# Four fetch buffers for the transposed scores, and the rest of the sum added in pieces

## The chip, the cores and the metric

The kernel runs on one core of one Trainium2 chip. The metric is the device time of one execution in microseconds (us), and lower is better. The engines are named as in the profile: PE (TensorE, the matmuls), DVE (VectorE), ACT (ScalarE), POOL (GpSimd) and SP (SyncE, which here only issues DMAs). Each engine has its own instruction queue and works through it in order.

## The reference

For x of shape [2, 2048, 256], the kernel computes attention and a gated feed-forward net (FFN) side by side on the same normalised input, and adds both to x:

```python
xn = _layernorm(x, axis=-1)
x = x + _L0_attn_ref(xn, Wq, Wk, Wv, Wo) + _L0_ffn_ref(xn, w1_w, w1_s, ..., w3_w, w3_s)
...
# attention: one head of width 256, causal
q, k, v = x @ Wq, x @ Wk, x @ Wv
attn = softmax(where(causal_mask, -max, q k^T) * 256 ** -0.5)
out = (attn v) @ Wo
...
# FFN, hidden width 1024; every weight is -1, 0 or 1, with a scale for each output
h = silu(tlin(x, w1)) * tlin(x, w2)
h = gelu(tlin(h, h1)); h = gelu(tlin(h, h2))
return tlin(h, w3)
```

## The kernel before, in words

**Tiles.** The 4096 rows are eight blocks n of TB = 512 rows, four (NB) for each batch, and each block is four tiles t of 128 rows; "(2,3)" is block 2, tile 3. Matmul operands are fp32r pairs: a rounded high half and the remainder as a low half, made by a copy on ACT (hi) and a subtraction on DVE or POOL (lo). A product is three products of halves.

**Attention.** Keys, queries and values of a block are made at L363 to L398 (the queries' projection is folded into wqk, the output's into wvo). `score` (L407 to L446) makes the scores of one tile against the blocks of its batch up to its own (PE L425, the mask L431), reduces the maxima (DVE L434, L440) and takes the exponential on ACT (L446), with the row sums. The tiles of batch 0 run from (3,3) down to (0,0), those of batch 1 upward from (4,0).

**Turning P.** The exponentials P must stand transposed ahead of the product with the values. A tile's P is cut into units of up to UK = 8 blocks of 128 columns. A unit of at least five goes "by blocks": DVE transposes 32x32 squares into one of two b tiles (L308), SP stores it to DRAM as d (L313), and four DMAs on SP fetch it back rearranged into a buffer e (L320). e comes from the pool bp with two buffers. `turn` (L470) then makes a piece pT of up to four blocks: ACT copies the hi half (L484), and DVE (even m) or POOL (odd m) subtracts for the lo half (L486). pT comes from the pool ptp, with LEAD + 2 = 4 buffers. Smaller units and the last tile are transposed on PE (L490) and split by ACT (L264) and DVE (L265). `weigh` (L505) multiplies by the values: hi products L518, lo products L523, into one of two PSUM tiles po; ACT L533 and DVE L537 (with L529 and L531) normalise into r, which is stored as r_d. `fetch_units` issues the fetches out of the list of stored units when `turn` reaches the first piece of a unit, and then one unit ahead. `weigh_steps` puts the turns LEAD = 2 pieces ahead of the weighing.

**Beside it.** x of batch 1 is loaded, normalised on POOL (L345, scale and offset from DVE L300) and turned in the same way by the b tiles (`turn_keys`, L351, so L308 and L313 also read x and write d_x). Between the steps, `beside` issues checks of the FFN's weights in small steps (DMA on ACT's queue L661; L590 to L607 on ACT and DVE, among them L603 and L605) and the sums of h1's quarters (`sum_up`, L611), which are gathered in the tile xh0 and stored to DRAM. Those begin after the last check of h2's signs. The pool xp has four buffers for x. At the end of attention the first parts of the FFN's gate are already made (`first_quarter`, L174 with ACT L182 and DVE L183).

**FFN.** `ffn_ternary` works on pairs of blocks. The gate (L174, L182, L183, splits L187 and L188) gives quarters B11, B12, B21 and B22. Each of the two hidden layers, `square`, is one Strassen step: seven products of 32 matmuls (L883), with sums and differences on DVE and POOL between them (L858, L863, L864, L922). The last product (L1044) gives y, and DVE adds it to "rest", x plus attention, and stores it. `rests_of` (L1004), called behind product 3 of the second layer, fetches attention's result and x (L1013, L1014) and adds them on POOL: L1015, one add of 128x1024 for each block, eight in all.

**What sets the order.** The order of issue in the source is not the order on the engines: each engine's queue is laid out by a scheduler from its own model of the times. `issue_after(x)` gives an edge to x only to instructions on x's own engine. The lists `looks`, `extra`, `TURN_KEYS` and the constants AHEAD, DELAY and LEAD say in which order the source issues.

```python
def fetch_units(until, more):
    while units and (more or until not in fetched):
        more = more and until not in fetched
        n, t, u, k, d = units.pop(0)
        e = bp.tile([P, UK * P], F32, tag="e", name=f"e_{n}_{t}_{u}")[:, : k * P]
        fetched[n, t, u] = fetch_blocks(d, k, e)
```

Of the kernel before, what the change touches and what calls it, by code (L numbers as in the profile page):

```python
# [20 lines left out]
P = 128  # L21
# [11 lines left out]
LOOKS_FROM = 3  # L33
LEAD = 2
WARM = 26
WARM_KEYS = 6
# [29 lines left out]
def attn_ffn_kernel(  # L66
# [124 lines left out]
    with ExitStack() as actx:  # L191
# [6 lines left out]
        sp = actx.enter_context(tc.tile_pool(name="sp", bufs=3))  # L198
        bp = actx.enter_context(tc.tile_pool(name="bp", bufs=2))
        ptp = actx.enter_context(tc.tile_pool(name="ptp", bufs=LEAD + 2))  # L200
        small = actx.enter_context(tc.tile_pool(name="small", bufs=4))
# [3 lines left out]
        xs, rstds, ks, qs, vs = {}, {}, {}, {}, {}  # L205
        turns = {"ps": 0, "b": 0, "q": 0}

        def in_turn(key, tiles):
            turns[key] += 1
            return tiles[(turns[key] - 1) % len(tiles)]  # L210

        def bank():
# [249 lines left out]

        def fetch_units(until, more):
            while units and (more or until not in fetched):
                more = more and until not in fetched
                n, t, u, k, d = units.pop(0)
                e = bp.tile([P, UK * P], F32, tag="e", name=f"e_{n}_{t}_{u}")[:, : k * P]
                fetched[n, t, u] = fetch_blocks(d, k, e)

        def turn(n, t, m):  # L470

            first = n - n % NB
            tiles = NT if m < n else t + 1
            w = tiles * P
            pT = ptp.tile([P, 2, TB], F32R, tag="pT", name=f"pT_{n}_{t}_{m}")
            state[n, t][m] = pT
            if by_blocks(n, t, m):
                u, at = divmod((m - first) * NT, UK)
                fetch_units((n, t, u * UK), at == 0)
                src = fetched[n, t, u * UK][:, ds(at, tiles)]  # L480
                hi, lo = (
                    pT[:, a, :w].rearrange("p (k i q) -> p k i q", k=tiles, q=Q) for a in range(2)
                )
                nc.scalar.copy(hi, src)  # L484
                engine = nc.gpsimd if m % 2 else nc.vector
                engine.tensor_tensor(lo, src, hi.bitcast(F32), ALU.subtract)  # L486
                return
            pt = ps_t.tile([P, TB], F32, tag="pt", name=f"pt_{n}_{t}_{m}")
            for j in range(tiles):
                nc.tensor.transpose(  # L490
                    pt[:, ts(j, P)], state[n, t]["s"][:, ds((m - first) * TB + j * P, P)], ident
                )
            hi_lo(pT[:, 0, :w], pT[:, 1, :w], pt[:, :w])
# [58 lines left out]
        def weigh_steps(g, until):  # L552

            steps = []
            while g < len(blocks) and blocks[g][0] <= until:
                while turned[0] <= min(g + LEAD, len(blocks) - 1) and (
                    turned[0] <= g or blocks[turned[0]][0] <= until + 1
                ):
                    b = blocks[turned[0]]
                    steps.append((0 if by_blocks(*b[1:]) else 2 * TB, lambda b=b: turn(*b[1:])))  # L560
                    turned[0] += 1
                _, n, t, m = blocks[g]
                steps.append((6 * TB if m < n else 6 * P * (t + 1), lambda b=blocks[g]: weigh(*b[1:])))
                g += 1
            return g, steps
# [63 lines left out]

        def item_signs(src):  # L630
            items.append(([src], [(0, lambda t: odd(t[0]))]))

# [17 lines left out]
        for k in range(HC):  # L650
            item_signs(h2[:, k, :])
        for c in range(HK):
# [132 lines left out]
    def ffn_ternary(actx):  # L785
# [83 lines left out]
        def square(layer, n, B, sets, last, beside):  # L869
# [6 lines left out]
            def product(step, out, start):  # L876
# [3 lines left out]
                for o in range(HK):  # L880
                    for c in range(HK):
                        for a in range(2):
                            nc.tensor.matmul(  # L883
                                out=out[o], lhsT=w[:, c, ts(o, P)], rhs=sets[right][c][:, a, :],
                                start=(start and c == 0 and a == 0), stop=(c == HK - 1 and a == 1),
                                skip_group_check=True,
                            )
                if step in beside:
# [57 lines left out]
            return C, nxt  # L946

        raw_h2 = {}

# [54 lines left out]
        def rests_of(n):  # L1004
# [4 lines left out]
            )  # L1009
            rests = {}  # L1010
            for i, m in enumerate((n + 1, n)):
                rests[m] = rest = rt[:, ts(i, NT), :]
                nc.sync.dma_start(out=rest, in_=r_d[m].rearrange("p (t d) -> p t d", d=D))  # L1013
                nc.sync.dma_start(out=xt[:, ts(i, NT), :], in_=rows_of(m))  # L1014
                nc.gpsimd.tensor_tensor(rest, rest, xt[:, ts(i, NT), :], ALU.add)  # L1015
            return rests

# [5 lines left out]
        for n in range(0, N, 2):  # L1023
# [6 lines left out]
            B, sets = square("h1", n, B, sets, False, later)  # L1030
            rests = {}
            B, sets = square("h2", n, B, sets, True, {3: lambda: rests.update(rests_of(n))})
            for m in (n + 1, n):
# [221 lines left out]
```

## Time and profile before

| what | value |
|---|---|
| three runs | 869.96, 867.01, 870.21 us (median 869.96) |
| profiled execution | 868.75 us, its span 866.9 us |
| mean granted PE clock | 0.998 |
| DVE, ACT, POOL busy | 74%, 58%, 27% of the span |
| attention, with the weights' checks | up to about 262 us |
| FFN, four pairs of blocks | from there to the end |
| DMA d<-b (stores of P's units) | 18 of 512 KB, median 3.9 us from issue to landing |
| DMA e<-d (fetches) | 72 of 128 KB, median 3.2 us |

A line of a timeline has the start in us from the beginning of the span, the length, the engine, the source line, the operation, output and inputs by the program's names (numbers left out), the shapes and the count of like instructions in a row; in brackets stands the idle time of the engine ahead of it and what ended that. A line of the waits has the engine and the line that waited, what released it, the total in us, the number of times and the longest. "PEclk" is the share of full clock that PE was granted.

### The profile page before, as it was taken

Reading aid. Unit: us, or ns where it says so; the run is one execution under the profiler, and the core shown is the slowest. Engines: PE = TensorE matmul, PEld = TensorE weight load, DVE = VectorE, ACT = ScalarE, POOL = GpSimd, SP = SyncE. Lnnn points to the kernel's source line nnn. Section 1 sums busy time; section 2 is a strip of 40 time slices with the busy share of each in tenths; the row PEclk is TensorE's granted clock in tenths of the full one; section 3 lists DMA queues with packets and bytes.
Section 4 is the critical chain, followed back from the end, with each engine's and each line's share of the span. In section 5 each row is a group of like instructions: output and inputs, shape, how many; then the busy total and the mean of one; then the engine's idle time right before and its main releaser. Section 6 shows DMA issues by size and latency. Waiting matters only on the chain.

```text
span 866.9 us, 12257 instructions
## 1 busy us (share of the span) xinstructions
PE 849.5 (98%) x4298; PEld 720.5 (83%) x4298; DVE 644.1 (74%) x1123; ACT 498.7 (58%) x881; POOL 234.7 (27%) x178
## 2 busy tenths in 40 slices
PE   9999799999999999999999999999999999999997
PEld 7988688988888878878988888988888898888887
DVE  6689685887965799986596596479478648848764
ACT  3456665655655466676257576436557635557671
POOL 3022823111111666630142150026024003502300
PEclk9999999999999999999999999999999999999999
DMA  8987899667881998754234444433444431144411
GB/s 276 361 233 233 249 314 291 222 234 231 286 283 51 389 403 282 285 194 152 93 132 143 144 146 141 144 116 109 145 145 145 145 135 58 49 146 146 146 49 53
DMA packets 62678, 162.51 MB, mean 187 GB/s; under 512 B 6545, under 2 KB 36369, under 8 KB 53265
## 3 DMA queue, kind: packets, MB, share of 16 engines
q1 hardware_dynamic: 57792, 145.14, 48.6%
q10 hardware_dynamic: 3728, 12.32, 4.6%
q0 software_dynamic: 1088, 4.19, 1.3%
q8 instruction: 36, 0.59, 0.3%
q14 instruction: 34, 0.27, 0.1%
HBM read 120.21 MB, written 47.71 MB: 194 GB/s over the span
## 4 chain that ended last, share of the span: by engine, by line
PE 83%; DVE 6%; DMA 5%; issue 2%; POOL 1%; ACT 1%; SPq 1%; DVEq 0%; ACTq 0%; POOLq 0%
PE ps_own L883 22%; PE ps L883 21%; PE ps L425 7%; PE ps L174 6%; PE ps_own L174 6%; PE po L518 4%; PE ps_own L1044 4%; PE ps L1044 4%; PE ps L398 3%; DMA e<-d 3%; DMA d<-b 2%; PE po L523 2%; PE ps L382 1%; POOL x L345 1%; DVE h_T L188 1%
## 5 line engine op out<-in xcount | busy, mean ns | idle before, releaser
L425 PE MATMUL ps<-k,q 128*128 128x512 f32 (+3 forms) x480 | 109.0, 366 | 0.4 <-ACT q L264 0.4
L425 PEld LDWEIGHTS ps<-k,q 128*128 128x128 f32 x480 | 82.0, 189 | 13.4 <-ACT q L264 1.2
L518 PE MATMUL po<-v,pT 128*128 128x512 f32 x272 | 79.1, 401 | 6.5 <-ACT pT L484 4.7
L486 POOL TENSOR_TENSOR pT<-e,pT 128x512 fp32r<-128x512 f32 (+3 forms) x30 | 36.8, 1229 | 140.1 <-ACT pT L484 102.6
L1015 POOL TENSOR_TENSOR rt<-rt,xt 128x1024 f32<-128x1024 f32 x8 | 21.9, 2758 | 170.3 <-issue 114.8
L904 ACT ACTIVATE k_h_u<-k_h_u,h_s_sb 128x512 f32<-128x512 f32 x64 | 45.9, 723 | 36.6 <-DVE k_h_u L903 36.0
L446 ACT ACTIVATE s<-s,low 128x1024 f32<-128x1024 f32 (+7 forms) x48 | 42.9, 895 | 30.8 <-DVE low L440 30.6
L518 PEld LDWEIGHTS po<-v,pT 128*128 128x128 f32 x272 | 47.3, 189 | 14.3 <-ACT pT L484 5.5
L863 POOL TENSOR_TENSOR k_h_u<-k_h_p,k_h_u 128x512 f32<-128x512 f32 x16 | 23.3, 1459 | 122.1 <-ACT q L187 106.0
L484 ACT CAST pT<-e 128x512 fp32r<-128x512 f32 (+3 forms) x60 | 32.8, 574 | 38.8 <-DMA e<-d 26.9
L434 DVE TENSOR_SCALAR_CACHE_REDUCE s<-ps 128x512 f32<-128x512 f32 (+3 forms) x80 | 47.2, 598 | 5.0 <-PE pt L490 3.1
L523 PEld LDWEIGHTS po<-v,pT 128*128 128x128 f32 x272 | 42.4, 188 | 6.8 <-DVE pT L486 0.7
L523 PE MATMUL po<-v,pT 128*128 128x256 f32 x272 | 46.2, 283 | 0.1
L188 DVE TENSOR_TENSOR q<-k_h_u,q 128x512 fp32r<-128x512 f32 x32 | 43.4, 1384 | 0.0
L308 DVE STREAM_TRANSPOSE b<-s 128x1024 f32<-128x1024 f32 (+3 forms) x30 | 33.4, 1124 | 8.3 <-ACT s L446 4.8
L922 POOL TENSOR_TENSOR k_h_p<-f_h_B,k_h_p 128x512 f32<-128x512 f32 x16 | 32.6, 2065 | 20.0 <-DVE h_h_T L188 20.0
L174 PE MATMUL ps<-xh,w_sb 128*128 128x512 f32 x144 | 36.4, 391 | 0.8 <-ACT b L182 0.8
L863 POOL TENSOR_TENSOR f_w_B<-f_w_B,f_w_B 128x512 f32<-128x512 f32 x16 | 26.8, 1692 | 33.1 <-DVE f_w_B L183 33.1
L903 DVE TENSOR_TENSOR k_h_u<-ps_own,k_h_u 128x512 f32<-128x512 f32 x32 | 21.7, 686 | 17.5 <-PE ps_own L883 17.4
L904 ACT ACTIVATE k_h_p<-k_h_p,h_s_sb 128x512 f32<-128x512 f32 x32 | 22.8, 722 | 19.3 <-DVE k_h_p L903 19.3
L903 DVE TENSOR_TENSOR k_h_u<-ps,k_h_u 128x512 f32<-128x512 f32 x32 | 22.0, 690 | 14.3 <-PE ps L883 14.3
L174 PE MATMUL ps<-xh1t,w_sb 128*128 128x512 f32 x128 | 31.8, 389 | 0.0
(178 smaller groups left out, 2206.2 us busy)
## 6 DMA issues: line engine op xcount, KB each, us to landing
w_h_S<-factors_h SPq DMA_DIRECT2D x32, 1024.0 KB, 4.8
w_h_A<-factors_h SPq DMA_DIRECT2D x24, 1024.0 KB, 4.8
d<-b SPq DMA_DIRECT2D x18, 512.0 KB, 3.9
e<-d SPq DMA_DIRECT2D x72, 128.0 KB, 3.2
xT_d<-k SPq DMA_DIRECT2D x8, 1024.0 KB, 6.0
stg<-in_ffn_h_w ACTq DMA_DIRECT2D x16, 512.0 KB, 4.8
r_d<-r SPq DMA_DIRECT2D x8, 512.0 KB, 4.3
factors_h<-xh SPq DMA_DIRECT2D x4, 1024.0 KB, 4.5
```

Of the source, the lines that this page charges most:

```text
L174: nc.tensor.matmul(out=p, lhsT=w[:, c, ts(o, P)], rhs=xh[:, c, a, :], start=(c == 0 and a == 0), stop=(c == DC - 1 and a == 1),)
L188: nc.vector.tensor_tensor(r[:, 1, :], f, r[:, 0, :].bitcast(F32), ALU.subtract)
L425: nc.tensor.matmul(out=ps[:, :w], lhsT=qs[n][:, c, a, ts(t, P)], rhs=ks[m][:, c, b, :w], start=(k == 0), stop=(m < n and k == 3 * DC - 1),)
L434: marks["DVE"] = nc.vector.tensor_scalar(st["s"][:, ds(at, w)], ps[:, :w], 1.0, None, ALU.mult, ALU.max, accum_out=st["tops"][:, m - first ...
L446: marks["ACT"] = nc.scalar.activation(st["s"][:, at], st["s"][:, at], AF.Exp, bias=low, accum_out=st["sums"][:, u // UK : u // UK + 1],).ins
L518: nc.tensor.matmul(out=st["po"], lhsT=pT[:, 0, ts(j, P)], rhs=vs[m][:, j, :, :], start=(m == first and j == 0), stop=False,)
L523: marks["PE"] = nc.tensor.matmul(out=st["po"][:, 0, :], lhsT=pT[:, 1, ts(j, P)], rhs=vs[m][:, j, 0, :], start=False, stop=(m == n and j == ...
L863: nc.gpsimd.tensor_tensor(B["B12"][i], B["B22"][i], B["B12"][i], ALU.subtract)
L883: nc.tensor.matmul(out=out[o], lhsT=w[:, c, ts(o, P)], rhs=sets[right][c][:, a, :], start=(start and c == 0 and a == 0), stop=(c == HK - 1 ...
L903: nc.vector.tensor_tensor(r[o], banks[o], r[o], ALU.add)
L904: nc.scalar.activation(C[k][o], r[o] if r else banks[o], AF.Gelu, scale=s[:, at : at + 1])
L1044: nc.tensor.matmul(out=ys[t][:, :D], lhsT=h[c][:, a, ts(t, P)], rhs=w3_sb[:, c, :], start=(c == 0 and a == 0), stop=(c == HC - 1 and a == 1),)
```

## The change

**Buffers.** The pool bp goes. There are now four fixed pT tiles (pT_tiles), two fixed e tiles (e_tiles), and two more e buffers, e_more, that are the two halves of xh0, in use until the last check of h2's signs has been issued (sums_begun). So four units can be fetched at once in the first part, then two. For blocks 6 and 7 (`wide`) a unit's buffer comes out of x's pool xp (four buffers), again with four at once, and the two e tiles serve as pT tiles five and six; there the turns are led by LEAD_WIDE = 4 pieces in place of 2.

**Fetches.** `fetch_units` fetches whenever fewer units are out than are allowed at once, and no longer only on a unit's first piece. A unit counts as out until its last piece has been issued in `turn`.

**Adds.** Each add of x and attention is cut into four of 128x256, 32 in all. Those of block n + 1 are issued in the source behind product 3, those of block n behind product 4, each with `issue_after` on the last matmul issued.

```diff
+LEAD_WIDE = 4
...
-        bp = actx.enter_context(tc.tile_pool(name="bp", bufs=2))
-        ptp = actx.enter_context(tc.tile_pool(name="ptp", bufs=LEAD + 2))
+        ptp = actx.enter_context(tc.tile_pool(name="ptp", bufs=1))
...
+        pT_tiles = [ptp.tile([P, 2, TB], F32R, name=f"pT_{i}") for i in range(LEAD + 2)]
+        e_tiles = [ptp.tile([P, UK * P], F32R, name=f"e_{i}") for i in range(2)]
+        e_more = [xh0[:, c].rearrange("p h t -> p (h t)") for c in range(DC)]
...
+        def wide(n, t):
+            return (n, t) >= (N - 2, 0)
+
+        def pT_tile(n, t):
+            tile = in_turn("pT", pT_tiles + (e_tiles if wide(n, t) else []))
+            return tile if len(tile.shape) == 3 else tile.rearrange("p (a t) -> p a t", a=2)
+
+        def units_at_once(n, t):
+            return 4 if wide(n, t) or not sums_begun else 2
+
+        def e_tile(n, t):
+            if wide(n, t):
+                return xp.tile([P, NT, D], F32, tag="x", name=f"e_{n}_{t}").rearrange("p t d -> p (t d)")
+            return in_turn("e", e_tiles + ([] if sums_begun else e_more)).bitcast(F32)
+
+        sums_begun = []
...
-        def fetch_units(until, more):
-            while units and (more or until not in fetched):
-                more = more and until not in fetched
+        def fetch_units():
+
+            while units and len(fetched) < units_at_once(*units[0][:2]):
                 n, t, u, k, d = units.pop(0)
-                e = bp.tile([P, UK * P], F32, tag="e", name=f"e_{n}_{t}_{u}")[:, : k * P]
-                fetched[n, t, u] = fetch_blocks(d, k, e)
+                fetched[n, t, u] = fetch_blocks(d, k, e_tile(n, t)[:, : k * P])
...
-            pT = ptp.tile([P, 2, TB], F32R, tag="pT", name=f"pT_{n}_{t}_{m}")
+            pT = pT_tile(n, t)
...
-                fetch_units((n, t, u * UK), at == 0)
+                fetch_units()
                 src = fetched[n, t, u * UK][:, ds(at, tiles)]
+                if at + tiles == fetched[n, t, u * UK].shape[1]:
+                    del fetched[n, t, u * UK]
...
-                while turned[0] <= min(g + LEAD, len(blocks) - 1) and (
-                    turned[0] <= g or blocks[turned[0]][0] <= until + 1
-                ):
+                while turned[0] < len(blocks):
                     b = blocks[turned[0]]
+                    lead = LEAD_WIDE if wide(*b[1:3]) and by_blocks(*b[1:]) else LEAD
+                    if turned[0] > g and (turned[0] > g + lead or b[0] > until + 1):
+                        break
...
-        def item_signs(src):
-            items.append(([src], [(0, lambda t: odd(t[0]))]))
+        def item_signs(src, last):
+            def signs(t):
+                if last:
+                    sums_begun.append(True)
+                odd(t[0])
+
+            items.append(([src], [(0, signs)]))
...
-                            nc.tensor.matmul(
+                            marks["PE"] = nc.tensor.matmul(
...
-                nc.gpsimd.tensor_tensor(rest, rest, xt[:, ts(i, NT), :], ALU.add)
-            return rests
+                adds[m] = [(r, r, xt[:, i * NT + t, :], ALU.add) for t in range(NT) for r in [rest[:, t, :]]]
+            return rests, adds
+
+        def add_rests(adds):
+
+            for k in adds:
+                with tc.issue_after(marks["PE"]):
+                    nc.gpsimd.tensor_tensor(*k)
...
-            B, sets = square("h2", n, B, sets, True, {3: lambda: rests.update(rests_of(n))})
+            rests, adds = {}, {}
+
+            def fetch_rests():
+                for a, b in zip((rests, adds), rests_of(n)):
+                    a.update(b)
+                add_rests(adds[n + 1])
+
+            B, sets = square("h2", n, B, sets, True, {3: fetch_rests, 4: lambda: add_rests(adds[n])})
```

More of the change, by code (lines that the diff above doesn't have):

```diff
@@ L205, in attn_ffn_kernel @@
         xs, rstds, ks, qs, vs = {}, {}, {}, {}, {}
-        turns = {"ps": 0, "b": 0, "q": 0}
+        turns = {"ps": 0, "b": 0, "q": 0, "pT": 0, "e": 0}
         def in_turn(key, tiles):
@@ L210, in in_turn @@
             return tiles[(turns[key] - 1) % len(tiles)]
+        pT_tiles = [ptp.tile([P, 2, TB], F32R, name=f"pT_{i}") for i in range(LEAD + 2)]
+        e_tiles = [ptp.tile([P, UK * P], F32R, name=f"e_{i}") for i in range(2)]
+        e_more = [xh0[:, c].rearrange("p h t -> p (h t)") for c in range(DC)]
+        assert UK * P == 2 * TB == NT * D
+        def wide(n, t):
[10 more added lines that the diff above has]
+        sums_begun = []
         def bank():
@@ L650, in attn_ffn_kernel @@
         for k in range(HC):
-            item_signs(h2[:, k, :])
+            item_signs(h2[:, k, :], k == HC - 1)
         for c in range(HK):
@@ L886, in product @@
                                 skip_group_check=True,
-                            )
+                            ).ins
                 if step in beside:
@@ L946, in square @@
             return C, nxt
+        marks = {}
         raw_h2 = {}
@@ L1009, in rests_of @@
             )
-            rests = {}
+            rests, adds = {}, {}
             for i, m in enumerate((n + 1, n)):
@@ L1030, in ffn_ternary @@
             B, sets = square("h1", n, B, sets, False, later)
-            rests = {}
-            B, sets = square("h2", n, B, sets, True, {3: lambda: rests.update(rests_of(n))})
+            rests, adds = {}, {}
+            def fetch_rests():
[3 more added lines that the diff above has]
+            B, sets = square("h2", n, B, sets, True, {3: fetch_rests, 4: lambda: add_rests(adds[n])})
             for m in (n + 1, n):
```

## The prediction

> **What bounds the kernel now.** I read the page first: TensorE (PE) is busy for all but 17 us, so a change pays only where PE stands idle, and costs only where it makes PE idle anew.
>
> ```profile
> PE 849.5 (98%) x4298; PEld 720.5 (83%) x4298; DVE 644.1 (74%) x1123; ACT 498.7 (58%) x881; POOL 234.7 (27%) x178
> ```
>
> Then the waits of PE (engine, line, released by; total us, times, longest): four entries hold 8.8 us, the only ones that the diff comes near.
>
> ```profile
> PE po L518 <- ACT pT L484: 4.7, 2, 2.6
> PE po L518 <- DVE r L537: 1.9, 1, 1.9
> PE ps_own L883 <- DVE h_h_T L188: 1.4, 2, 1.0
> ...
> PE ps L174 <- ACT b L182: 0.8, 1, 0.8
> ```
>
> Then the timeline around them (start, length, instruction; in brackets the idle time ahead). Stalls 1, 2 and 3 start the weighing of a unit too late:
>
> ```profile
> 89.21 1.21 PE L518 MATMUL po<-v,pT 128*128 128x512 f32 x4 [2.04 <-ACT pT L484]
> ...
> 98.45 0.74 PE L523 MATMUL po<-v,pT 128*128 128x256 f32 x4
> ...
> 105.74 1.20 PE L518 MATMUL po<-v,pT 128*128 128x512 f32 x4 [2.61 <-ACT pT L484]
> ...
> 138.44 1.19 PE L518 MATMUL po<-v,pT 128*128 128x512 f32 x3 [1.89 <-DVE r L537]
> 139.43 2.88 PE L398 MATMUL ps<-wvo,k 128*128 128x256 f32 x12
> ```
>
> Their causes are on the other queues: SP's fetches (each waits until an e buffer is free), POOL, ACT, DVE.
>
> ```profile
> 80.18 4.59 SPq L320 DMA_DIRECT2D e<-d  x8
> ...
> 98.43 3.64 SPq L320 DMA_DIRECT2D e<-d  x8
> ```
> ```profile
> 86.69 10.45 POOL L345 TENSOR_SCALAR x<-x,rstd,off 128x256 f32<-128x256 f32 x14 [2.86 <-DVE off L300]
> 97.12 1.28 POOL L486 TENSOR_TENSOR pT<-e,pT 128x512 fp32r<-128x512 f32 x1
> ```
> ```profile
> 97.69 1.28 ACT L446 ACT_TABLE_LOAD   x1 [3.69 <-DVE low L440]
> 98.99 1.15 ACT L446 ACTIVATE s<-s,low 128x1024 f32<-128x1024 f32 x1
> ```
> ```profile
> 134.96 1.25 DVE L308 STREAM_TRANSPOSE b<-x 128x1024 f32<-128x1024 f32 x1 [4.26 <-DMA d<-b]
> ...
> 137.91 0.48 DVE L537 SCALAR_TENSOR_TENSOR r<-po,inv,y 128x256 f32<-128x256 f32 x1
> ```
>
> The unit of tile (3,0) was stored by 69.8, but its fetch went out at 80.18 and landed at 88.4: stall 1. The unit of (2,3) was stored by 82.5, but fetched at 98.43, because its buffer was read last by the lo step (L486) at 97.12, and that stood behind fourteen normalisations of x: stall 2. Stall 3 is r (L537) behind a transpose which waited 4.26 us for a store to leave its b buffer. In the FFN PE runs at 0.227 us per matmul (7.25 per 32) and stops near 370 only, where DVE's splits and POOL's two-input operations go by turns, whole instruction for whole instruction:
>
> ```profile
> 365.86 6.29 DVE L188 TENSOR_TENSOR h_h_T<-k_h_p,h_h_T 128x512 fp32r<-128x512 f32 x3
> ```
> ```profile
> 367.06 2.85 POOL L1015 TENSOR_TENSOR rt<-rt,xt 128x1024 f32<-128x1024 f32 x1
> ```
>
> I count in PE's **lag**: the time at which a matmul starts, less the pitches of all ahead of it. In the trace it is 8.3 at 98.45, 11.6 behind stall 2, 11.95 ahead of stall 3, 15.8 behind the slow stretch that follows it, 16.4 at 200 and 18.2 at 262. The sum is made against the profiled execution (868.75 us, span 866.9); the median of the three runs, 869.96, is 1.2 above it, so I add 1.2 at the end. The order of instructions on each engine is taken from the built program.
>
> **A: four buffers, up to the lo product of (3,0).** The fetch of (3,0) no longer waits for a buffer: out at about 71.7, landed by 77 (5 us as others). So the DMA of stall 1 goes; ACT's queue then ends its copy at 87.6 (table load, root and a check stand ahead), and of 2.2 us 0.8 stay. But a few products on, PE needs the lo half of (3,0)'s second piece, from POOL. There it now stands behind fifteen L345 instead of fourteen: 86.1 (off half a microsecond earlier) + 15 × 0.746 (10.45 / 14) + 1.28 = 98.6. In the trace it ended at 98.40. What stall 1 gives is waited away here; with 0.2 of matmuls that move ahead, lag **+0.4**. The other side: if POOL gets through before 95, −2.
>
> **B: stall 2 and what takes its place.** The fetch of (2,3) comes some 20 us earlier, so 11.6 − 8.3 = 3.3 of lag go. But in the built order ACT's copy of (2,3)'s second piece stands ahead of the exp of (2,0), and it writes a pT tile that PE must first have read. So: PE done with (3,0)'s lo product 99.2; copy 0.62; table load 1.28; exp 1.15: 102.3 where it was 100.14. Then DVE: transpose 1.25 (103.7), its store 4.24 (a store issued at 103.89 landed at 108.13): 107.9. The next transpose (of (1,3)) wants the same b buffer, and DVE keeps its order: 1.23, a check L605 1.23, then the lo half of PE-turned pT, L265, 0.68, which PE needs for (2,3): 111.0. PE would be there at 106.3 with nothing missing: 4.7 lost, some 1.8 of it already at the hi product. Net: +0.4 − 3.3 + 4.7 = **+1.8** including A. Stores landed after 3.6 to 6.6 us at such places, so B alone may be 0.6 less or 2.4 more; if DVE isn't held, A and B together go down to −5.3.
>
> **C: stall 3.** In the new order r of tile (2,0) is ahead of the transpose of x_7: 15.8 − 11.95 = 3.8 go (1.9 of idle time, some 0.25 around it, and 1.7 of slow clock). What is late next: the lo half of q (L265) and, for its bank, the values' product L398/L425 behind that same transpose: 0 to 3, I take 1.0, the side of the 1.9 row. The clock: granted 0.50 from 138.99 for 3.41 us, after 1.89 us of idle time (twelve L398 took 2.88 us, where eleven took 1.42 before); idle times of 2.04 and 2.61 drew none. One window costs 1.7; with B's and C's new waits I take half of one, 0.85. Net **−1.95**; ends −3.8 and +1.
>
> The Trainium skill ("TensorE: Matmul & The Clock Gate", Part 1: The HAM clock gate) has the rate halved only after an idle window of about 3.4 us. The length of the slow stretch agrees with its window of 3413 ns, the 1.89 us of idle time don't agree with its threshold. By the rule neither B nor C would draw a window, and the forecast would be 0.85 lower.
>
> **D: 262.** The third quarter of the gate stands 14 us of matmuls later in PE's order, so that its wait for ACT (0.76, with 0.15 around it) goes: **−0.9**. Ends 0 and −0.9.
>
> **E: adds in quarters.** 32 adds instead of 8. In POOL's order they stand where the whole ones stood (ahead of T4 in pair 0, at the gate in the others): the edge from the PE instruction moves nothing on POOL. Each should take about 2.9/4 = 0.73 and hold DVE as long. DVE's three splits at 365.86 then go by turns with 1.7 + 0.73 + 0.73 in place of 1.68 + 2.85 + 1.72; 3 us are won on DVE, so both PE stalls there (0.59 + 1.13 with their rims) go: **−1.7**. Pairs 1 to 3 show no PE stall at their adds: 0. Ends 0 (DVE meets other quarters instead) to −1.7; at worst a quarter costs what a 128x256 normalisation does, 0.746: 32 × 0.746 = 23.9 against 21.9 on the page, 2 us more of POOL, a quarter of it in pair 0: +0.5.
>
> **F: lead of four, six pT and x's buffers in blocks 6 and 7.** From 200 to 262 the lag grows by 1.8 in crumbs under 0.15 us, so there is nearly nothing to win: **0**. PE covers it; if the earlier copies on ACT come ahead of an exp as in B, +1; at best −1. Fetches issued early on SP stand behind no buffer any more, so the stores behind them move forward, not back: 0.
>
> **Sum:** 1.8 − 1.95 − 0.9 − 1.7 = −2.75: 866.0 profiled, **867.2** on the median's scale.
>
> **The rivals.** R1, the waits really go: POOL ends its normalisations early enough or the store of (2,0) lands before DVE wants its buffer. For it: all four fetches are 9 to 20 us early; against it: the built order on POOL and ACT. Worth 3.3 (B) + 3.8 (C) + 0.9 (D) + 1.2 of E = 9.2: 868.75 − 9.2 + 1.2 = **861**, at best 858. R2, slower: DVE stands behind b buffers. There are still two b buffers, units come closer together, and DVE, in order, holds everything else. Stores at 6.4 instead of 4.2 add 2.2 in B; at x_7's transposes 3 instead of 1; and both idle times draw a slow window (1.7 each). B 1.8 + 2.2 + 1.7 = 5.7; C −3.8 + 3 + 1.7 = 0.9; D and E −2.3 (half a stall stays): +4.3: **874.3**, range 871 to 877. It decides once these stores take over 5 us; the store that held DVE at 134.96 took 6.4, that at 103.89 4.2, and the share of DMA time rises from .70 to .94 there. R3, the change doesn't do what it says: POOL's adds stay in place and free nobody, and earlier fetches meet the same late POOL and ACT steps: **869**, 868 to 870.5.
>
> **How the numbers follow.** Forecast (864 to 870.5) 0.42; R1 0.27; R2 0.21; R3 0.10. 0.5% (4.35 us) is about what a measurement of this kernel can tell from no change. Faster than 865.6: R1 whole and 0.08 of the forecast, 0.35. Slower than 874.3: somewhat over half of R2, 0.12. The rest 0.53. The range 860 to 874 leaves out about 0.08 of R1 and 0.12 of R2.
>
> **What would show it.** A: e<-d of (3,0) issued near 72, and PE's lag near 8.7 at the first lo product behind POOL's fifteenth normalisation. B: a DVE transpose near 108 waiting about 4 us on a store, and PE idle twice, 1.8 and about 3. C: no PE wait on r; granted clock below 1.0 in that stretch or not. D: no wait on L182. E: quarter adds near 0.73, and the three splits in about 3.2 us. Wrong if the DMA waits come back (e<-d after 20 us of queueing), if ACT puts the exp first after all, or if anything in the FFN, where PE is at its pitch, gets slower.

## The result, and the profile after

The changed kernel is **slower, by a little over half a per cent**: 874.12 us against 868.37 us (seven runs each), ratio 1.0067 [1.0038, 1.0096]. In a second set of runs it was 873.83 against 869.89, ratio 1.0044 [1.0025, 1.0064]. Ratios leave one execution out, one of e1's twelve, which took 1548.15 us at a granted clock of 0.55. The predicted 867.2 is 6.9 us too low, and 874.12 lies just outside the range of 860 to 874. The profiled execution was the fastest of the seven: 870.82 us, span 869.0, mean clock 0.996. A second profile (873.44 us, span 871.7) is used beside it, because single stalls differ between the two.

The busy times are those of before, save POOL's, which are 7.6 us up. So PE does the same work, and the time is lost where it stands idle. The engines' line and the chain's shares, from the page of the changed kernel:

```profile
PE 849.9 (98%) x4298; PEld 721.0 (83%) x4298; DVE 642.9 (74%) x1123; ACT 499.4 (57%) x881; POOL 242.3 (28%) x202
...
PE 79%; DMA 10%; DVE 6%; issue 1%; ACT 1%; SPq 1%; POOL 0%; ACTq 0%; DVEq 0%
```

Where the time went is seen from PE's lag, the prediction's measure: the start of a matmul less the pitches of all ahead of it (here the median pitch of its shape in the profile before). The three stretches are cut in PE's work time, a matmul's start less its lag, so that each holds the same amount of work in every kernel. 72 to 156 of work time is about 76 to 170 us of the span, most of the first part; 156 to 276 is about 170 to 292 us before and 170 to 297 us after, blocks 5 to 7 and the gate's first matmuls; from there to the end of PE's work it is the FFN. Stretches of lag are given by work time below, lines of profiles by the span's. (The prediction's lags, with other pitches, stand 1.5 to 3.6 us higher: 8.3 at 98.45 is 6.8 here.) "Order of before" are the kernel before and e1 below, which has the same order of instructions in attention.

| profile | 72 to 156 | 156 to 276 | FFN | sum |
|---|---|---|---|---|
| before | +10.0 | +2.1 | +3.8 | 15.9 |
| order of before again (e1) | +13.5 | +2.6 | +1.0 | 17.1 |
| changed | +10.6 | +6.8 | +0.7 | 18.1 |
| changed again (e6) | +11.8 | +7.9 | +1.5 | 21.2 |

Two things stand out. The first stretch varies by 1 to 4 us between two profiles of one order, and the change is inside that spread. The second stretch, from 156 to 276, where I had predicted −0.9 (D) and 0 (F), grows by about 5 us more than before, in both profiles. The waits of PE from 155 to 275 us, changed kernel (engine and line that waited, releaser, total us, times, longest); the profile of before had only D's wait on L182 there (0.8):

```profile
PE po L544 <- ACT pT L510: 2.3, 3, 1.5
PE ps L450 <- DVE s L459: 0.6, 1, 0.6
PE po L544 <- DVE r L563: 0.6, 1, 0.6
PE ps L450 <- DVE v L290: 0.5, 1, 0.5
```

(L510, L512, L544, L549 and L450 of the changed kernel are L484, L486, L518, L523 and L425 of before.) The larger single stalls, from PE's timeline of the changed kernel:

```profile
88.12 1.20 PE L544 MATMUL po<-v,pT 128*128 128x512 f32 x4 [1.22 <-ACT pT L510]
...
96.03 1.43 PE L450 MATMUL ps<-k,q 128*128 128x512 f32 x5 [2.71 <-DVE s L459]
...
111.70 1.22 PE L549 MATMUL po<-v,pT 128*128 128x256 f32 x4 [2.58 <-DVE pT L290]
...
268.77 1.20 PE L544 MATMUL po<-v,pT 128*128 128x512 f32 x4 [1.55 <-ACT pT L510]
```

So stalls 2 and 3 are gone, stall 1 is shorter, and three stalls of like size stand at other places. The four sum to 8.1 us, where stalls 1 to 3 and D's wait were 7.3: the large stalls hardly moved in sum. In blocks 5 to 7 the waits of 4.0 us in all are the one of 1.55 and pieces of about half a microsecond.

### The profile page after: what moved, and what is told of

The parts are those of the page before. It is cut to its first block, busy times and chain, and to the rows that moved or that the text cites. A ratio compares the mean times of both kernels' runs of the same rounds, so it can differ in the third digit from the quotient of the medians.

```text
span 869.0 us, 12292 instructions
## 1 busy us (share of the span) xinstructions
PE 849.9 (98%) x4298; PEld 721.0 (83%) x4298; DVE 642.9 (74%) x1123; ACT 499.4 (57%) x881; POOL 242.3 (28%) x202
## 4 chain that ended last, share of the span: by engine, by line
PE 79%; DMA 10%; DVE 6%; issue 1%; ACT 1%; SPq 1%; POOL 0%; ACTq 0%; DVEq 0%
PE ps_own L915 23%; PE ps L915 23%; PE ps L175 7%; PE ps_own L175 6%; DMA d<-b 5%; PE ps_own L1089 4%; PE ps L1089 4%; PE ps L450 3%; PE po L544 3%; DMA e<-d 2%; PE ps L423 2%; PE ps L407 2%; SPq L345 1%; PE po L549 1%; DVE b L333 1%
## 5 line engine op out<-in xcount | busy, mean ns | idle before, releaser
L450 PE MATMUL ps<-k,q 128*128 128x512 f32 (+3 forms) x480 | 110.0, 367 | 4.3 <-DVE s L459 3.4
L450 PEld LDWEIGHTS ps<-k,q 128*128 128x128 f32 x480 | 81.9, 188 | 18.3 <-DVE s L459 4.3
L1055 POOL TENSOR_TENSOR rt<-rt,xt 128x256 f32<-128x256 f32 x32 | 31.7, 1022 | 165.3 <-issue 114.8
L544 PE MATMUL po<-v,pT 128*128 128x512 f32 x234 | 68.8, 403 | 3.8 <-ACT pT L510 3.5
L512 POOL TENSOR_TENSOR pT<-e,pT 128x512 fp32r<-128x512 f32 (+3 forms) x18 | 21.6, 1207 | 110.1 <-ACT pT L510 97.2
L544 PEld LDWEIGHTS po<-v,pT 128*128 128x128 f32 x234 | 40.6, 189 | 11.6 <-ACT pT L510 4.8
L549 PEld LDWEIGHTS po<-v,pT 128*128 128x128 f32 x234 | 36.9, 191 | 7.8 <-DVE pT L290 2.9
L549 PE MATMUL po<-v,pT 128*128 128x256 f32 x234 | 40.2, 285 | 2.6 <-DVE pT L290 2.6
L510 ACT CAST pT<-e 128x512 fp32r<-128x512 f32 (+3 forms) x36 | 19.3, 577 | 26.5 <-DMA e<-d 17.6
L189 DVE TENSOR_TENSOR h_h_B<-f_h_B,h_h_B 128x512 fp32r<-128x512 f32 x32 | 21.4, 717 | 14.8 <-ACT h_h_B L188 14.8
L935 DVE TENSOR_TENSOR k_h_u<-ps,k_h_u 128x512 f32<-128x512 f32 x32 | 21.9, 690 | 13.4 <-PE ps L915 13.4
```

The lines of the kernel that those rows point to most:

```text
L189: nc.vector.tensor_tensor(r[:, 1, :], f, r[:, 0, :].bitcast(F32), ALU.subtract)
L450: nc.tensor.matmul(out=ps[:, :w], lhsT=qs[n][:, c, a, ts(t, P)], rhs=ks[m][:, c, b, :w], start=(k == 0), stop=(m < n and k == 3 * DC - 1),)
L544: nc.tensor.matmul(out=st["po"], lhsT=pT[:, 0, ts(j, P)], rhs=vs[m][:, j, :, :], start=(m == first and j == 0), stop=False,)
L549: marks["PE"] = nc.tensor.matmul(out=st["po"][:, 0, :], lhsT=pT[:, 1, ts(j, P)], rhs=vs[m][:, j, 0, :], start=False, stop=(m == n and j == ...
L935: nc.vector.tensor_tensor(r[o], banks[o], r[o], ALU.add)
```

## The experiments

The theory after the result (T1): the fixed pT tiles change the order of ACT's and DVE's work in blocks 5 to 7, and that order costs the time. Its rivals: the four early fetches cost it through other waits (T2); the quartered adds cost it (T3); x's buffers and six pT in blocks 6 and 7 cost it (T4). Each run is given as median, ratio to the kernel before in the same set with its interval, and growth of lag from 156 to 276 of work time.

### One part at a time: e1 to e5, and the change again

**e1**, the kernel before with only the adds cut in four:

```diff
-                nc.gpsimd.tensor_tensor(rest, rest, xt[:, ts(i, NT), :], ALU.add)
+                for t in range(NT):
+                    nc.gpsimd.tensor_tensor(rest[:, t, :], rest[:, t, :], xt[:, i * NT + t, :], ALU.add)
```

> The kernel before with the adds cut into quarters and nothing else. Theory (the loss is in attention, the adds gain): PE's stalls near 370 (0.59 + 1.13 us) go, as they did in the trace of the changed kernel: 1.7 to 2 us faster than before, all of it in the first pair of blocks, and quarter adds of about 1 us each. Rival (32 adds hold DVE longer than 8): no faster than before, new PE waits at the gates of pairs 1 to 3.

**e2**, the changed kernel without x's buffers and six pT in blocks 6 and 7; **e3**, without four at once in the first part; **e4**, without either, so that of the change the fixed tiles, the new rule for fetches and the adds are left. The first edit is that of e2, the second that of e3, and e4 has both:

```diff
-            return (n, t) >= (N - 2, 0)
+            return False
```
```diff
-            return 4 if wide(n, t) or not sums_begun else 2
+            return 4 if wide(n, t) else 2
-            return in_turn("e", e_tiles + ([] if sums_begun else e_more)).bitcast(F32)
+            return in_turn("e", e_tiles).bitcast(F32)
```

> The changed kernel without the treatment of blocks 6 and 7 (x's buffers, six pT tiles, lead of four); its order is that of the changed kernel up to block 6. Theory (the last part of attention loses the 5 us): PE's lag from block 6 on grows by 0.5 to 2 us instead of 5, the time is 3 to 5 us below the changed kernel, about 869 to 871. Rival (the loss comes from crowded DMAs in the first part): no more than 1 us below the changed kernel, 873 to 875.

> The changed kernel with two units fetched at once in the first part, in place of four (blocks 6 and 7 as changed). Theory (early fetches crowd the stores of d, and DVE stands behind a b buffer): the PE stall near 93 (2.7 us, DVE behind the store of (2,1)) goes, the stalls of before behind late fetches come back, so that up to 120 us PE's lag is that of before within 1 us; the time stays 3 to 5 us above before, because of blocks 6 and 7. Rival (the first part alone makes it slower): at the time of before or below.

> The changed kernel with both taken back: two units at once everywhere, two e and four pT tiles, lead of two; what is left is the fixed tiles, the rule for fetching and the quartered adds. Theory: 1 to 2 us below before, about 867, from the adds. Rival (the new rule for fetching or the new order loses by itself): above before.

**e5**, the kernel before with four fixed pT tiles and two fixed e tiles in place of the two pools, and nothing else (whole adds, old rule for fetches); **e6**, the changed kernel again:

```diff
+        pT_tiles = [ptp.tile([P, 2, TB], F32R, name=f"pT_{i}") for i in range(LEAD + 2)]
+        e_tiles = [ptp.tile([P, UK * P], F32, name=f"e_{i}") for i in range(2)]
...
-                e = bp.tile([P, UK * P], F32, tag="e", name=f"e_{n}_{t}_{u}")[:, : k * P]
+                e = in_turn("e", e_tiles)[:, : k * P]
...
-            pT = ptp.tile([P, 2, TB], F32R, tag="pT", name=f"pT_{n}_{t}_{m}")
+            pT = in_turn("pT", pT_tiles)
```

> The kernel before with fixed pT and e tiles in place of the pools, the same number of each, the old fetches and whole adds. In the built order this alone moves some 150 lines on PE and 190 on DVE, as many as the version with both parts taken back; fixed e tiles alone or the new rule for fetching alone move none. Theory (with fixed pT tiles ACT may write the hi half while the lo products still read the other half, the scheduler lays out attention anew, and the new layout is the worse one): 3 to 4 us slower than before, 873 to 875, the loss at the stalls of the first part and from block 5 on. Rival (the layout is as good; the loss of the version with both parts taken back came with the adds): within 1 us of before.

> The changed kernel once more, for a second profile and a second interval. Theory (the first part waits for stores of d that land early or late, execution by execution): 4 to 6 us above before, and in the first part stalls of other sizes at the same places (DVE behind a b buffer near 93 and 108), so that the lag at the end of the first part differs by 1 to 4 us from the first profile, while from block 5 on it grows by 6 us as there. Rival (both profiles alike within 1 us at each stage: no such spread).

| run | parts of the change in it | us | ratio | 156 to 276 |
|---|---|---|---|---|
| e1 | adds | 868.71 | 0.9990 [0.9967, 1.0013] | +2.6 |
| e5 | fixed tiles | 873.04 | 1.0040 [1.0012, 1.0068] | +6.9 |
| e4 | fixed tiles, adds | 873.69 | 1.0036 [1.0011, 1.0061] | +5.6 |
| e2 | and four early fetches | 872.90 | 1.0033 [1.0012, 1.0054] | +7.8 |
| e3 | e4 and x's buffers, six pT | 873.01 | 1.0035 [1.0013, 1.0058] | +4.8 |
| e6 | all | 873.83 | 1.0044 [1.0025, 1.0064] | +7.9 |

The fixed tiles alone bring the kernel to where the whole change is. No other part moves the time by what its interval can tell, in either direction: T3 falls, T4 falls, and T2 isn't needed. The gains that were expected of e2 (869 to 871) and e4 (about 867) didn't come. In the built program the fixed e tiles alone move no instruction on any engine, and the new rule for fetches alone moves none; four fixed pT tiles move about 150 lines of PE's order and 190 of DVE's. The built orders of e4 and e5 differ only in POOL's adds. What is left of e5 is the pT tiles. They also lie at other addresses than before, which no run separates from the order; ACT's and POOL's busy times don't show it (498.3 and 234.9 us in e5, 498.7 and 234.7 before).

### Early fetches without fixed pT tiles: e7

**e7**, the kernel before, pool of pT kept, with four units at once in the first part and quartered adds:

```diff
+            if not sums_begun and turns["e"] % 4 in (0, 3):
+                return e_more[turns["e"] % 4 // 3]
+            return bp.tile([P, UK * P], F32, tag="e", name=name)
...
+            while units and len(fetched) < (2 if sums_begun else 4):
```

> The kernel before with four units fetched at once in the first part (two e buffers from the pool, two in h1's sums' memory) and quartered adds, but pT from its pool as before and nothing for blocks 6 and 7. Theory (fixed pT tiles do the harm): at or below before, 866 to 870. Rival (the early fetches themselves do it, by crowding the stores that DVE waits for): 3 us or more above before, with DVE waiting over 10 us for stores in all.

877.64 us, ratio 1.0092 [1.0059, 1.0124], lag +16.1 from 72 to 156 (to 176 us of the span) and +7.2 from 156 to 276. The largest waits of PE from 60 to 156 us in e7:

```profile
PE pt L500 <- DVE pT L274: 2.8, 1, 2.8
PE ps L434 <- DVE s L443: 2.1, 1, 2.1
PE po L528 <- ACT pT L494: 1.7, 1, 1.7
```

So T2 isn't wrong on its own ground: with the pool, early fetches cost more than with fixed tiles. The two parts don't add up (0.4% and 0.9% alone, 0.4 to 0.7% together), so what is measured is each kernel's order as a whole, not a price of a part. The stores held DVE for 6.6 us only, where over 10 had been expected.

### A third b tile: e8

**e8**, e2 with a third b tile for P's and x's stores, and three units at once in the first part:

```diff
-            return 4 if wide(n, t) or not sums_begun else 2
+            return 2 if sums_begun else 3
...
+            b = in_turn("b", [t.rearrange("p i t -> p (i t)") for t in b_tiles] + ([] if sums_begun else e_tiles[1:]))[:, : k * P]
```

> The changed kernel without the treatment of blocks 6 and 7, and in the first part with three b buffers and three units at once (one of the e tiles serves as third b). Theory (DVE behind b buffers is what the first part loses): DVE's waits for stores of d fall from about 7 us to under 3, PE's lag at 140 is 1.5 us or more below that without the third buffer, and the time is 2 us or more below the version without the treatment of blocks 6 and 7, some 870. Rival (other waits take its place): DVE's waits for stores go, the time stays within 1 us of that version, 872 to 874.

873.46, ratio 1.0040 [1.0017, 1.0062], where e2 had 1.0033. DVE no longer waits for any store in the first part, and the time stays: other waits take the place. DVE's largest, from 60 to 155:

```profile
DVE pT L512 <- ACT pT L510: 7.8, 4, 3.7
DVE e L333 <- ACT s L471: 6.0, 2, 5.1
```

The stores that hold DVE (rival R2's mechanism) are there in the changed kernel, 7.1 us in all from 60 to 155 us, but taking them away, with one fetch at once fewer, gives nothing back.

### x's turn and the gate: e9 to e12

In all profiles with the `TURN_KEYS` of before, the last block of x (x_7: stored by SP behind the units, fetched, copied by ACT at L388) lands at 148.4 to 154.9 us. **e10** begins x's turns earlier, **e9** puts the gate's third quarter back to where it stood in PE's order, **e11** does both, and **e12** is e1 with e10's turns. The first edit is that of e10 and e12 (e11 has [8, 9, 11, 13]), the second that of e9 and e11:

```diff
-TURN_KEYS = [8, 10, 12, 14]
+TURN_KEYS = [8, 9, 10, 11]
```
```diff
-            if (n, t, m) == (N - 1, NT - 1, N - 2):
+            if (n, t, m) == (N - 1, NT - 2, N - 4):
```

> The changed kernel with the third quarter of the gate issued ahead of tile (7,2)'s weighing: in the built order its eight matmuls (1.8 us) stand just ahead of the products of (7,2), and nothing before them moves. Theory (the change took away the cover of the wait for (7,2)'s unit): the PE wait of 1.5 us near 268 goes, and the time is 1 to 2 us below the changed kernel, 872 to 873. Rival (another wait takes its place, since ACT's copies of (7,2) are late by more): the time stays, 873 to 875.

> The changed kernel with x_5, x_6 and x_7 turned at the tiles 9, 10 and 11 in place of 10, 12 and 14. Theory (x_7, which goes through the b buffers, DRAM and SP behind the units, lands at 151 to 154 us in all ten profiles so far, however early PE is, and what the first part gains is given back there): x_7 lands before 146, PE's lag grows by less than 0.7 us from 140 to 172 where it grew by 1.3 and 3.6 in the two profiles of the changed kernel, and the time is 1 to 3 us below it. Rival (the DMA engines are full from 87 to 145 us, so that an earlier x_7 makes the units later): the first part takes that much longer, and the time is that of the changed kernel or above.

> The changed kernel with the gate's third quarter ahead of (7,2) and x_5, x_6 and x_7 turned at the tiles 9, 11 and 13, one tile earlier each. Theory (two separate losses): 2 to 4 us below the changed kernel, 870 to 872, about the time of before. Rival (the new layout loses in crumbs elsewhere): 873 or above.

> The kernel before with quartered adds and x_5, x_6 and x_7 turned at the tiles 9, 10 and 11. Theory (before reaches block 6's keys only when x_7 has landed anyway): no gain from it, within 1.5 us of the one with quartered adds alone, 868 to 871, or some us above if the new layout leaves waits from block 5 on. Rival (x_7 holds before as well): 2 us or more below, under 867.

e9 874.58, 1.0049 [1.0029, 1.0070]; e10 872.11, 1.0022 [1.0006, 1.0038]; e11 874.36, 1.0045 [1.0025, 1.0066]; e12 872.83, 1.0046 [1.0025, 1.0068]. So e11, with both edits, gains nothing. ACT's copies of x_7, in the changed kernel and in e10:

```profile
152.07 1.15 ACT L388 CAST k<-x 128x512 fp32r<-128x512 f32 x2 [3.27 <-DMA x<-d_x]
```
```profile
142.81 1.14 ACT L388 CAST k<-x 128x512 fp32r<-128x512 f32 x2
```

The wait for x_7 goes in e10, and the whole kernel is perhaps 2 us better than the changed one (its interval overlaps that of e6). But the lag from 140 to 172 of work time still grew by 1.5 where under 0.7 was expected, as PE then waits 1.1 us at 155 us for the copy of a fetched unit. The theory that x_7 takes back the early fetches is half borne out. e12 shows that the same step in the order of before gains nothing and costs 0.46%.

In e9 the wait moved, as the rival had it: the gate's matmuls now wait 1.03 us for a PSUM bank, which ACT (L183) is late to free, and a later product waits 0.51 us for a hi half from ACT (L289). From PE's timeline of e9:

```profile
267.23 2.12 PE L175 MATMUL ps<-xh,w_sb 128*128 128x512 f32 x8 [1.03 <-ACT b L183]
...
275.98 1.21 PE L544 MATMUL po<-v,e 128*128 128x512 f32 x4 [0.51 <-ACT e L289]
```

### One wait of T1 by itself: e13 to e16

What another order can do is seen at one place. ACT's timeline, before and then changed: before, the exps of (6,1) and (6,2) are through by 208.7, and only then come the copies of (6,0)'s unit; in the changed kernel the two copies stand ahead of the exp of (6,2), and wait 3.61 us for the fetch.

```profile
207.01 1.14 ACT L446 ACTIVATE s<-s,low 128x1024 f32<-128x1024 f32 x1
...
208.14 0.60 ACT L446 ACTIVATE s<-s,low 128x384 f32<-128x384 f32 x1
...
208.98 0.62 ACT L484 CAST pT<-e 128x512 fp32r<-128x512 f32 x1
```
```profile
208.60 0.49 ACT L471 ACTIVATE s<-s,low 128x256 f32<-128x256 f32 x1
...
212.80 1.14 ACT L510 CAST e<-e 128x512 fp32r<-128x512 f32 x2 [3.61 <-DMA e<-d]
213.85 1.15 ACT L471 ACTIVATE s<-s,low 128x1024 f32<-128x1024 f32 x1
...
215.59 0.46 ACT L559 ACTIVATE y<-po,inv 128x256 f32<-128x256 f32 x1
```

The exp comes 6.8 us later, with y behind it; PE waits 0.60 at 216.85 for r (which reads y) and 0.64 at 222.36 for a PSUM bank. Lag from 196 to 212 of work time grows by 2.1 here, 2.1 in e6 and 2.5 in e2, but by 0.2 in e3, e4, e5 and e7, nearly as without any change (0.1): this wait needs the fixed tiles and the early fetches together, and the fixed tiles alone don't bring it. **e13** (from the changed kernel) and **e14** (from e10) give the first of the two copies an edge to that exp; **e15** is e2 with e10's turns, **e16** is e14 with `DELAY_BLOCKS` at 45000 in place of 42000:

```diff
+                    exps[n, t] = marks["ACT"]
...
-                nc.scalar.copy(hi, src)
+                with ExitStack() as behind:
+                    if (n, t, m) == (N - 2, 0, N - 4):
+                        behind.enter_context(tc.issue_after(exps[n, t + 2]))
+                    nc.scalar.copy(hi, src)
```

> The changed kernel with ACT's first copy of (6,0) put behind the exponential of (6,2). Theory (the copy holds the exponential, y and r while it waits for its fetch): the PE waits near 216 and 222 (0.8 us each) go, PE's lag grows by less than 0.7 us from 196 to 212 in place of 2.1, and the time is 1 to 2 us below the changed kernel. Rival (the fetch itself is what PE needs there, and the order on ACT doesn't matter): the lag grows by 1.5 us or more, and the time stays.

> The one with x turned early, with the same copy put behind the exponential of (6,2); PE's order doesn't change at all. Theory: the lag grows by less than 0.7 us from 196 to 212 in place of 2.2, and the time is 1 to 2 us below that one, about that of before (870 to 871). Rival: no change, 872.

> The changed kernel with x turned early and without x's buffers and six pT tiles for blocks 6 and 7. Theory (that part of the change neither gains nor loses by itself): within 1.5 us of the one with x turned early, 870.5 to 873.5. Rival (x's buffers are what makes blocks 6 and 7 late): 2 us or more below it, at or under 870.

> x turned early, the copy behind the exponential, and the delay between a tile's scores and its weighing raised from 42000 to 45000 in the source's own count. Theory (from block 5 on fetches land a few microseconds after ACT wants them, so 3000 more, about 1.1 us of matmuls, cover some of it): 0.5 to 1.5 us below the one with the copy behind the exponential. Rival (the layout is a new one, with other waits): 1 us or more above.

e13 878.65, 1.0104 [1.0079, 1.0130]; e14 871.55, 1.0024 [1.0006, 1.0043]; e15 871.51, 1.0030 [1.0006, 1.0053]; e16 872.02, 1.0033 [1.0012, 1.0054]. The test failed to isolate the wait. Only the first copy moved; the second stayed ahead of the exp and waited itself, as ACT's timeline of e14 shows:

```profile
211.26 0.62 ACT L514 CAST e<-e 128x512 fp32r<-128x512 f32 x1 [2.96 <-DMA e<-d]
211.78 1.15 ACT L471 ACTIVATE s<-s,low 128x1024 f32<-128x1024 f32 x1
```

PE's wait of 0.64 at 222.30 was still there, to the hundredth. The lag grows by 2.0 more here than before; whether taking the wait away would give that time back stays open. e13 even lost 0.6% more than the changed kernel (1.0104 against 1.0044, in another set), lag +10.9 from 156 to 276. e16's longer delay gains nothing over e14, where 0.5 to 1.5 us were expected. e15 against e10 shows again that x's buffers and six pT do nothing.

### Is any other order slower? e17 and e18

If each new order costs 0.4%, the pT tiles are only an occasion. **e17** and **e18** are e1 with another `DELAY_BLOCKS` (45000 and 41000), which moves 186 and 116 lines of PE's order and leaves the pools:

```diff
-DELAY_BLOCKS = 42000
+DELAY_BLOCKS = 45000
```

> The kernel before with quartered adds and the delay of the units raised from 42000 to 45000 (186 lines move on PE, 164 on DVE; no buffer changes). Theory (the order of before is a good one, and a new order costs a few microseconds whatever its reason): 2 to 5 us above before. Rival (fixed pT tiles do the harm): within 1.5 us of before, like the one with quartered adds alone.

> The same with the delay lowered to 41000 (116 lines move on PE, 90 on DVE). Theory: 2 to 5 us above before. Rival: within 1.5 us of before.

e17 869.61, ratio 1.0000 [0.9980, 1.0019], lag +6.8 from 72 to 156 and +5.0 from 156 to 276; e18 868.13, ratio 0.9982 [0.9961, 1.0003], +11.5 and +1.5. Waits of PE from 155 to 275 us in e5 (fixed tiles), then in e18 (pools):

```profile
PE po L520 <- ACT pT L486: 2.1, 3, 1.3
PE po L525 <- DVE pT L267: 1.0, 1, 1.0
PE ps L174 <- DVE s L436: 0.8, 1, 0.8
PE ps L427 <- DVE v L267: 0.2, 1, 0.2
```
```profile
PE ps L425 <- DVE s L434: 0.3, 1, 0.3
```

A new order isn't slower as such. But e12, also with pools, lost 0.46%, so fixed tiles aren't the only way to a bad one. No version was measurably faster than the kernel before; e1, e17 and e18 are as fast and are faster than the changed kernel.

## Why the prediction was wrong, by its steps

**F failed, and it decides.** It gave the stretch of blocks 6 and 7 a price of 0: nothing to win, and "PE covers it; if the earlier copies on ACT come ahead of an exp as in B, +1". The runs: from 156 to 276 the lag grows by 4.2 to 5.8 more than in the two profiles of the order of before, and fixed tiles alone give +3.1 us (e5: 873.04 against 869.89). What F priced, the larger lead and the extra buffers, was rightly put at nothing (e2, e15; with the lead back at two, no line of the built order moves). What no term of the sum priced was that the pT tiles are fixed. The hi copy of a piece may then start before the lo products have read the other half of its tile, which 6 of 54 copies in the changed profile do, all before 126 us, and PE's, DVE's and ACT's queues are laid out anew. Blocks 5 and 6 had been taken unread, because their stalls of before were under 0.15 us. A stretch with no stall has nothing to win, but everything to lose. That the fixed tiles cost the time is shown (e5, e4). Where they cost it is seen in part: from 236 to 252 of work time, which is the end of block 7 with the gate's first matmuls, the lag grows by 2.7 to 3.9 in the changed kernel, e2, e3, e4, e5 and e6, against 1.2 and 1.8 in the order of before (0.1 in e18, but 2.8 in e17). Which of the queues costs how much isn't shown, as e13 and e14 didn't take a wait away.

**D was wrong in sign.** The wait on L182 went, as predicted. But at the place that the gate's matmuls left, the same work of ACT is still in PE's way: ACT makes the copies for the next products behind the gate's table load and activation (2.0 us together, right behind an exp), and PE waits 1.55 at 268.77 for the first copy. ACT's timeline of the changed kernel:

```profile
266.23 1.28 ACT L183 ACT_TABLE_LOAD   x1
267.52 0.69 ACT L183 ACTIVATE b<-ps,w_s_sb 128x512 f32<-128x512 f32 x1
268.11 2.06 ACT L510 CAST pT<-e 128x512 fp32r<-128x512 f32 x4
```

No fetch is late there: ACT stands idle ahead of none of these. From 236 to 252 of work time the lag grows by 2.75 against 1.2. e9 shows that there was no gain to be had by putting the gate's matmuls back either.

**A was right about the fetch, not about POOL.** The fetch of (3,0) went out at 70.31 (predicted 71.7); its first unit had landed by 74.8 and its second by 78.7 (predicted: 77); 1.22 of the stall was left (0.8; in the second profile 2.35, again for ACT's copy). But the lo half that was to come at 98.6 and to take this gain back was through at 96.88: POOL's fifteen normalisations took 8.99 us, 0.60 each where 0.746 had been counted. PE didn't wait for it. It stood for something that no term has. SP's issues, changed kernel:

```profile
80.92 3.66 SPq L345 DMA_DIRECT2D e<-d  x8
85.48 0.34 SPq L338 DMA_DIRECT2D d<-b  x1
```

The store of (2,1) landed at 93.66, 8.2 us after its issue (4.9 before), and DVE's transpose of x_4 waited 1.76 for its b tile, with PE's next bank behind it: the stall of 2.71 at 96.03. In the second profile the store landed after 5.5 us, and the stall isn't there. In all three profiles eight fetch DMAs were issued just ahead of that store, so the new fetch order doesn't explain the difference; its cause stays open. F had said of the early fetches that "the stores behind them move forward, not back": this one was issued 0.3 us earlier than before and landed 3.0 us later.

**B was right in place and cause.** DVE's timeline of the changed kernel:

```profile
108.68 1.25 DVE L333 STREAM_TRANSPOSE b<-s 128x1024 f32<-128x1024 f32 x1 [2.22 <-DMA d<-b]
109.84 1.18 DVE L632 SCALAR_TENSOR_TENSOR stg<-stg 128x1024 f32<-128x1024 f32 x1
...
110.96 0.69 DVE L290 TENSOR_TENSOR pT<-pt,pT 128x512 fp32r<-128x512 f32 x1
```

The lo half was to be through at 111.0 and was at 111.65. DVE stood 2.22 us for the store (predicted about 4), PE 2.58 (about 3); of the other wait of PE, 1.8 at the hi product, 0.17 came. In the second profile PE stood 1.22 at the same place.

**C: the stall on r went; the clock cost a whole window, not half.** PE waits for no r near 138. But the granted clock falls to 0.50 behind B's idle time, from 111.36 for 3.41 us. That the length of the idle time didn't tell (2.58 us drew a window here, 2.71 us at 96.03 none) has a pattern behind it, which the prediction lacked. In all 20 profiles the granted clock changes only on a grid of 3.413 us, and what goes with a slow step is PE's idle time inside the step ahead of it. Steps of the changed kernel (us, then busy time and count of PE, PEld, DVE, ACT, POOL; granted clock, DMA share, GB/s):

```profile
94.29:97.70 3.41, 1.67 (x7) 1.41 (x8) 3.41 (x5) 1.57 (x2) 3.41 (x5) 1.00 0.38 154
97.70:101.12 3.42, 3.42 (x18) 2.70 (x18) 3.42 (x11) 1.90 (x2) 1.32 (x3) 1.00 0.64 190
107.95:111.36 3.41, 1.16 (x6) 0.83 (x5) 2.68 (x4) 1.00 (x3) 0.53 (x1) 1.00 0.40 121
111.36:114.77 3.41, 3.07 (x10) 2.77 (x11) 3.41 (x9) 1.10 (x2) 0.00 (x0) 0.50 1.05 383
```

The 2.71 us lie across two steps, 0.97 and 1.74 us, and the next step has the full clock; of the 2.58 us 2.24 lie in one step, and the next has half. Before, the 2.61 us of stall 2 lay as 1.73 and 0.88, the 1.89 us of stall 3 in one step. Over all profiles, between PE's first full clock and the end of its work, each of the 26 slow steps follows a step with 1.61 to 3.27 us of idle time, and no step with 1.8 us or more is followed by the full clock; between 1.61 and 1.75 both occur. The Trainium skill ("TensorE: Matmul & The Clock Gate", Part 1: The HAM clock gate) says that the windows run freely and don't reset, which agrees with the grid; that it takes an idle window of about 3.4 us is not what these rows show: about half of one was enough.

A to C together were to bring the lag 0.15 lower; from 72 to 156 it grew by 10.6 and 11.8, against 10.0 and 13.5. No gain and no loss can be told there.

**E was mis-sized.** A quarter takes 1.19 us beside DVE's splits, not 0.73, which it takes only at other places. POOL's group on the page (total, mean ns) and a stretch of its timeline:

```profile
L1055 POOL TENSOR_TENSOR rt<-rt,xt 128x256 f32<-128x256 f32 x32 | 31.7, 1022 | 165.3 <-issue 114.8
```
```profile
371.89 4.63 POOL L1055 TENSOR_TENSOR rt<-rt,xt 128x256 f32<-128x256 f32 x4
```

They sum to 31.7 us against the 21.9 of the whole ones (23.9 was to be the worst), and three splits beside them took 4.08 (3.2 predicted, 6.29 before). POOL and DVE go by turns: beside the first four quarters DVE's L896 took 1.22 us, and 0.68 right after them, so that a quarter and a DVE instruction pass in 1.2 us together. PE's stalls near 370 did go; but they are also absent in e5, with whole adds that start earlier and meet other instructions of DVE. So whole adds don't always bring them, and what one execution showed was counted as the kernel's. The time of e1, 0.9990 [0.9967, 1.0013], shows no gain, though its interval doesn't exclude the 1.7 us (0.2%) that E promised.

**The rivals.** R1 (861) named waits that did go, but not what replaced them. R2 gave 874.3, and its side was right; its mechanism was not, and the hit of its number is luck. DVE waited for stores of P 7.1 and 5.1 us from 60 to 145 us in the two changed profiles, no more than in those of the order of before (7.6 and 10.8), and e8 took these waits away without a gain. R3 (869) is where e1, the adds alone, came out; of the whole change it was wrong, since the fetches did come early.

## What to carry to other kernels

Where a scheduler lays out the queues, changing how buffers are declared is an edit to every queue that touches them: read the whole new order, above all where the old one has no stall. Undo the parts one by one before believing in any of them; here the part that seemed a detail carried the loss, and no other part's effect could be told from nothing. A stall in one profiled execution of a kernel that is busy for 98% may be that execution's own: look at a second profile before costing it as a gain.

## What the runs showed of the hardware

- The same store of 512 KB, with eight fetch DMAs issued just ahead of it each time, landed 8.2 and 5.5 us after its issue in two profiles of the changed kernel, and 4.9 before.
- Cutting a two-input POOL operation in four made it dearer in sum when DVE works beside it: 4.62 us for four 128x256 in place of 2.85 for one 128x1024.
- PE was granted half rate for 3.41 us behind idle times of 1.89 and 2.58 us, and full rate behind 2.04, 2.61 and 2.71. The granted clock changed only on a grid of 3.413 us, and half rate followed a step of the grid in which PE had been idle for 1.61 us or more, without exception from 1.8 (26 slow steps in 20 profiles).
